# Attention masks of the first of 16 graphs: written by the scalar engine, or added by TensorE

## The chip, the core and the metric

The kernel runs on one NeuronCore of a Trainium2 chip. The metric is the device time of one execution in microseconds (us). A profile is one such execution, recorded instruction by instruction.

TensorE (PE) multiplies a stationary operand with a moving one and writes to the accumulation memory, PSUM. ScalarE (ACT), VectorE (DVE) and GpSimd (POOL) do elementwise work, and SP issues most transfers.

## What is computed

There are 16 graphs (`B`) of 1024 nodes with 128 features. Four residual layers follow each other, each of the form x = x + layer(relu(layernorm(x))): a dilated GraphSAGE layer, softmax attention with a mask, graph attention (GAT), and a graph convolution (GCN). The change concerns the second layer, with four heads of 32 features:

```python
scores = jnp.einsum('chqd,chkd->chqk', q, k) * SCALE
scores = scores + jnp.log(jnp.maximum(edge_weight, EPS))[:, None, :, :]
attn = jax.nn.softmax(scores, axis=-1)
out = jnp.einsum('chqk,chkd->chqd', attn, v)
```

`edge_weight` is the adjacency matrix of zeros and ones, and EPS is 1e-8. A pair without an edge thus gets log(1e-8) = -18.42 more than one with an edge. The kernel adds 16 times the adjacency to the scores and multiplies by SIGMA = 18.42/16 inside the exponential; a constant common to all pairs cancels in the softmax.

## The kernel before, in words

The first part of the kernel (dilation and the three GraphSAGE convolutions) runs up to about 1560 us of the profile. The rest is `attentions_plain`, which takes all 16 graphs through the other three layers. It is written as seven Python generators, one for each kind of work:

- `matrices` (line 1308) loads a graph's adjacency row block by row block, turns it into fp8 (line 1318), and checks its symmetry with small matmuls (lines 1329 and 1331) and an activation (line 1335).
- `before` (line 1343) finishes the first layer (matmuls at line 1365, whose inputs `hT_a` and `h_a` come from HBM by SP's queue), normalises, transposes (line 1291), and makes the queries and keys (line 1383 on PE, 1385 on ACT) and the values (line 1303 on PE, 1387 on ACT).
- `attend` (line 1397) makes the masked scores and their exponentials.
- `values` (line 1434) multiplies the exponentials with the values and with ones (line 1452), takes the reciprocal of the sums (line 1458) and projects.
- `positive` and `gat` (lines 1470 and 1507) are the graph attention: it starts with a normalisation (line 1282) once the graph's softmax attention is done, builds 32 masks on DVE (line 1503) and sums on PE (lines 1563 and 1578).
- `gcn` (line 1602) is the last layer.

For each graph `attend` runs 16 iterations: two halves of the queries (512 columns each) times eight blocks of 128 keys. One iteration fills the tile `s` ("t" in the profile), which is 128 x 4 heads x 512 in fp32. It takes four of PSUM's banks, one for each head, and there is only one such tile. The steps of an iteration are: ACT writes 16 times the adjacency block into all four heads (line 1416); PE adds the scores of the four heads on top (line 1421, four matmuls of 32 rows which lie in different row groups of the array); ACT takes two exponentials of two heads each into `es` ("e" in the profile, two buffers; line 1429). The next iteration's mask can only be written when both exponentials have read `s`. Before the first iteration 16 small identity matmuls (line 1405) write all of `s` once, so that the accumulating matmuls of line 1421 add to what ACT wrote.

`values` (line 1452) issues eight matmuls for each iteration, four with the values and four with ones, in column groups of the array. All other matmul outputs go through two banks named "sum".

The order of the instructions on each engine is made when the program is built. `in_order` (line 1658) steps through the generators. Each yields the engine of its next step, the planned time of the step, and the time at which its inputs are there; the planner always takes the step that can start first, and on a tie prefers the other engines to PE and then the generator with the least PE time done for its weight. The planned time of a mask is 1.9 us on ACT, of a group of scores 1.1 us on PE, of an exponential 1.07 us on ACT, of one iteration's value matmuls 1.95 us on PE. Each engine then works its list strictly in that order and waits wherever an input is late. `matrices` and `before` run ahead of `attend` by up to one graph; so while the first graph is in its attention, the second is being prepared and no GAT or GCN work exists yet.

Of the kernel before, what the change touches and what calls it, by code (L numbers as in the profile page):

```python
# [8 lines left out]
BF16 = mybir.dt.bfloat16  # L9
F8 = mybir.dt.float8e4  # L10
I32 = mybir.dt.int32
AF = mybir.ActivationFunctionType
ALU = mybir.AluOpType
# [5 lines left out]
P = 128  # L19
NB = N // P  # L20
H, HD = 4, 32
HN = N // 2
# [1191 lines left out]
def attentions_plain(tc, x, spill, final, ready_weights, adj, deg, trouble, eye, out, scores, bound, reach):  # L1214
    nc = tc.nc
    with ExitStack() as ctx:
        cp = ctx.enter_context(tc.tile_pool(name="f_const", bufs=1))
# [12 lines left out]
        ident = cp.tile([P, P], F32, name="ident")  # L1230
        nc.sync.dma_start(ident, eye)
        ident16 = cp.tile([P, P], BF16, name="ident16")
# [2 lines left out]
        nc.vector.tensor_scalar(minus16, ident, -1.0, None, op0=ALU.mult)  # L1235
        ones16 = cp.tile([3, P], BF16, name="ones16")
        nc.vector.memset(ones16, 1.0)
        minus_half = cp.tile([P, NB], F32, name="minus_half")
        nc.vector.memset(minus_half, -0.5)
        ones = cp.tile([P, HD], F32, name="ones_hd")  # L1240
# [17 lines left out]
        A, ready, done = {}, {}, {"before": 0, "attend": 0, "gat": 0, "gcn": 0}  # L1258
# [138 lines left out]
        def attend():  # L1397

            last = 0.0


            s = pss.tile([P, H, HN], F32, name="t")
            for hd in range(H):
                for c in range(4):
                    nc.tensor.matmul(s[:, hd, c * P:(c + 1) * P], ident16, ident16, start=c == 0, stop=c == 3)
            n = 0
            for b in range(B):
                while b not in ready or b not in A:
                    yield
                t, xt, qT, kT, va = ready[b]  # L1410
                for hf in range(2):
                    cols = slice(hf * HN, (hf + 1) * HN)
                    for k in range(NB):
                        e = yield "ACT", 1.9, last, 0

                        nc.scalar.activation(s, A[b][:, k, None, cols].to_broadcast([P, H, HN]), AF.Copy, scale=16.0)  # L1416
                        e = yield "PE", 1.1, max(e, t), 0

                        for hd in range(H):
                            r = slice(hd * HD, (hd + 1) * HD)  # L1420
                            nc.tensor.matmul(s[:, hd], kT[r, k * P:(k + 1) * P], qT[r, cols], start=False, stop=True,  # L1421
                                             skip_group_check=True)
                        while n > 1 and n - 2 not in taken:
                            yield
                        es = ep.tile([P, H, HN], F32, name="e")
                        e = max(e, taken.get(n - 2, 0.0))
                        for hd in range(0, H, 2):
                            e = yield "ACT", 1.07, e, 0
                            nc.scalar.activation(es[:, hd:hd + 2], s[:, hd:hd + 2], AF.Exp, scale=SIGMA)  # L1429
                        exps[n] = es, e  # L1430
                        last = e
                        n += 1
# [215 lines left out]
        with tc.manual_schedule(engines=set(ENGINES.values())):  # L1648
            in_order([(0, 4.0, matrices()), (3, 18.0, before()), (0.5, 17.6, attend()), (3, 34.0, values()), (1, 2.0, positive()),
                      (1, 54.0, gat()), (2.5, 17.0, gcn())], {"sum": 2})  # L1650
# [97 lines left out]
def whole(tc, x, adj, nodemask, chunk_mats, chunk_mask, eye, sel, p, out):  # L1748
    nc = tc.nc
    with tc.tile_pool(name="dram", bufs=1, space=DRAM) as dp, tc.tile_pool(name="keep", bufs=1) as kp:  # L1750
# [19 lines left out]
        with tc.tile_pool(name="final", bufs=1) as fp:  # L1770
            final = [fp.tile([P, D], F32, name=f"final{i}") for i in range(3)] + [fp.tile([3, D], BF16, name="final_row")]
            with tc.tile_pool(name="early", bufs=1) as yp, tc.tile_pool(name="c_adj", bufs=2) as ap, \
                    tc.tile_pool(name="c_x", bufs=2) as xp:
                ident = yp.tile([P, P], F32, name="ident")
                nc.sync.dma_start(ident, eye)
                minus_half = yp.tile([P, NB], F32, name="minus_half")
                nc.vector.memset(minus_half, -0.5)
                h0 = xp.tile([P, NB, D], F32, name="xt")
                attention_weights(tc, ap, ident, ready_weights, *weights)
                dilate_plain(tc, adj, eye, kept, rdeg, unsettled, norm_first(tc, x, yp, h0, minus_half))  # L1780
                convolutions_plain(tc, x, ident, ap, xp, h0, minus_half, kept, rdeg, spill, final, *layer0)
            attentions_plain(tc, x, spill, final, ready_weights, adj, deg, trouble, eye, out, scores, bound, reach)
# [45 lines left out]
```

## Time and profile before

| | |
|---|---|
| Median of three runs | 3990.11 us (3984.71 to 3998.74) |
| Profiled execution | 3983.57 us |
| Its span | 3981.8 us |
| Mean granted TensorE clock | 0.932 of full |
| PE, ACT, DVE busy | 86%, 60%, 63% of the span |
| Mask activations (line 1416) | 256, 1883 ns each, first at 1609.6, last at 3825.5 |
| Score matmuls (line 1421) | 1024, recorded as 2048, 663 ns each |
| Exponentials (line 1429) | 512, 1022 ns each |
| Value matmuls (line 1452) | two kinds of 1024 each, recorded as 2048, 620 and 599 ns each |

A row of the profile names line, engine and operation, the tiles (output, arrow, inputs), the shape, and how many there were. Behind the bar stand the busy time in all, the mean of one in ns, and the idle time of the engine just before such instructions with what ended it. An fp32 matmul is recorded as two instructions. The four matmuls of a row or column group run at the same time, so their mean durations can't be multiplied by their number. A line of the timeline gives start, duration, engine, line, operation, tiles, shape and count; a bracket tells how long the engine had been idle and what it waited for.

The second part of the kernel has three stretches: a start (about 1555 to 1725 us) with only the preparation and attention of graph 0, the preparation of graph 1 and its first iterations; a middle, up to about 3830, in which the attention of one graph runs beside the GAT and GCN of earlier ones; and an end, in which GAT and GCN of the last graph remain.

### The profile page before, as it was taken

What the parts mean: (1) busy time and instruction counts of PE and PEld (TensorE: products, weight loads), DVE (VectorE), ACT (ScalarE), POOL (GpSimd) and SP (SyncE); (2) the same over time, 40 slices, a digit from 0 to 9 for tenths busy, and PEclk for the clock granted to TensorE, in tenths of its full rate; (3) what the DMA queues carried; (4) which work ended last, traced back from release to release, by engine and by line L of the source; (5) the groups of instructions that cost most, each with busy time, mean ns of one, the idle gap of its engine ahead of it and who ended that gap; (6) DMA issues with size and microseconds to landing.
All of it is one profiled execution on the core that took longest, in us unless ns stands there. A gap on an engine that the chain in (4) does not pass through costs nothing.

```text
span 3981.8 us, 65726 instructions
## 1 busy us (share of the span) xinstructions
PE 3429.2 (86%) x26692; PEld 1966.6 (49%) x26692; DVE 2528.4 (63%) x4782; ACT 2398.6 (60%) x3961; POOL 790.9 (20%) x680
## 2 busy tenths in 40 slices
PE   4888887899999986789899898998989899889775
PEld 2556565445555565335554544544444454454333
DVE  4988784553344444247775777677687686777656
ACT  3778764453333345776677676767757767776540
POOL 6545421210010011102121111111111101210110
PEclk9989986999999997999999998998999989999887
DMA  9632223443333314211221122122122112111000
GB/s 107 41 21 16 12 79 122 160 170 122 127 128 129 129 61 141 79 59 49 65 86 59 49 75 76 37 75 79 41 67 81 48 50 85 56 58 49 27 17 17
DMA packets 182499, 293.20 MB, mean 74 GB/s; under 512 B 77468, under 2 KB 124456, under 8 KB 173992
## 3 DMA queue, kind: packets, MB, share of 16 engines
q1 hardware_dynamic: 91944, 221.69, 17.1%
q0 software_dynamic: 79728, 24.66, 7.6%
q10 hardware_dynamic: 10512, 42.54, 2.7%
q8 instruction: 211, 3.46, 0.4%
q14 instruction: 104, 0.85, 0.1%
HBM read 287.98 MB, written 51.19 MB: 85 GB/s over the span
## 4 chain that ended last, share of the span: by engine, by line
PE 60%; DVE 20%; ACT 8%; DMA 5%; issue 3%; POOL 3%; ACTq 0%; SPq 0%; POOLq 0%; DVEq 0%
PE g L1040 12%; PE acc L1452 10%; PE sum L1578 9%; PE t L1421 5%; PE sum L1632 4%; PE sum L1563 4%; DVE pm L1503 3%; DMA rows<-in_adj_dram 2%; DVE rows L882 2%; PE sum L1365 2%; PE o L1089 2%; DVE r L835 2%; PE o L1090 2%; ACT e L1429 1%; PE sum L1383 1%
## 5 line engine op out<-in xcount | busy, mean ns | idle before, releaser
L1429 ACT ACTIVATE e<-t 128x1024 f32<-128x1024 f32 x512 | 507.9, 1022 | 485.8 <-PE t L1421 467.9
L1503 DVE SCALAR_TENSOR_TENSOR pm<-dst,minus,A 128x1024 fp8e4<-128x1024 f32 x512 | 675.5, 1348 | 8.4 <-DMA dst<-scores 8.3
L1040 PE MATMUL g<-C,parts 128*128 128x512 fp8e4 x2304 | 523.9, 382 | 15.9 <-DVE aggT L1042 10.0
L1416 ACT ACTIVATE t<-A 128x2048 f32<-128x2048 fp8e4 x256 | 482.0, 1883 | 3.9 <-ACT dst L1483 0.3
L1578 PEld LDWEIGHTS <-pm 128*128 128x128 fp8e4 x4096 | 346.6, 98 | 187.0 <-issue 165.0
L1578 PE MATMUL sum<-parts,pm 128*128 128x198 bf16 x4096 | 399.7, 251 | 26.1 <-DVE pm L1503 16.4
L1452 PE MATMUL acc<-e,va 128*32 128x512 f32 x2048 | 331.6, 620 | 41.1 <-ACT e L1429 38.2
L1040 PEld LDWEIGHTS <-parts 128*128 128x128 bf16 x2304 | 224.0, 99 | 264.1 <-issue 9.6
L1421 PE MATMUL t<-qT,kT 32*128 32x512 f32 x2048 | 303.5, 663 | 30.6 <-ACT t L1416 30.3
L1452 PE MATMUL acc<-e,ones_hd 128*32 128x512 f32 x2048 | 318.4, 599 | 0.0
L1581 DVE TENSOR_REDUCE pos<-sum 128x132 f32<-128x396 f32 x256 | 144.8, 566 | 201.1 <-PE sum L1578 200.5
L1563 PE MATMUL sum<-parts,A 128*128 128x396 bf16 x1024 | 212.1, 352 | 44.9 <-DVE parts L1555 24.0
L1042 DVE TENSOR_TENSOR aggT<-g,rdb 128x512 f32<-128x512 f32 x96 | 66.1, 690 | 270.6 <-PE g L1040 270.5
L1632 PE MATMUL sum<-A,gparts 128*128 128x512 fp8e4 x768 | 176.3, 382 | 24.9 <-ACT gparts L1615 17.6
L1045 POOL TENSOR_TENSOR nrm<-nrm,minus_half 128x8 f32<-128x8 f32 x48 | 78.6, 1638 | 594.3 <-DVE nrm L1103 585.9
L835 DVE TENSOR_TENSOR r<-ya,both 128x512 bf16<-128x512 f16 x184 | 140.4, 777 | 87.9 <-ACT ya L832 87.0
L1275 POOL TENSOR_TENSOR ln_st<-ln_st,minus_half 128x8 f32<-128x8 f32 x48 | 86.1, 1794 | 510.5 <-DVE ln_st L1273 348.4
L1563 PEld LDWEIGHTS <-A 128*128 128x128 fp8e4 x1024 | 94.7, 99 | 183.7 <-issue 106.6
L882 DVE SCALAR_TENSOR_TENSOR rows<-y,thirty,rows 128x1024 fp8e4<-128x1024 f16 x128 | 168.5, 1324 | 24.0 <-ACT y L874 23.5
L1100 ACT ACTIVATE sq<-o 128x512 f32<-128x512 f32 x96 | 55.2, 596 | 204.7 <-PE o L1093 125.1
L872 PE MATMUL big<-tri,rows 128*128 128x256 fp8e4 (+3 forms) x896 | 175.6, 318 | 0.6 <-ACT y L874 0.4
L885 POOL TENSOR_TENSOR own<-rows,lower 128x256 bf16<-128x256 fp8e4 x128 | 109.1, 862 | 334.2 <-DVE rows L882 201.2
(291 smaller groups left out, 6779.7 us busy)
## 6 DMA issues: line engine op xcount, KB each, us to landing
a<-in_adj_dram SPq DMA_DIRECT2D x128, 512.0 KB
C<-kept SPq DMA_DIRECT2D x48, 1024.0 KB
dst<-scores SPq DMA_DIRECT2D x64, 512.0 KB
rdb<-rdeg SPq DMA_DIRECT2D x48, 512.0 KB
spill<-hT ACTq DMA_DIRECT2D x48, 512.0 KB
kept<-rows ACTq DMA_DIRECT2D x16, 1024.0 KB
h_a<-spill SPq DMA_DIRECT2D x64, 256.0 KB
hT_a<-spill SPq DMA_DIRECT2D x16, 512.0 KB
```

The costliest lines, as they stand in the source:

```text
L835: nc.vector.tensor_tensor(r, ya, both[:, 1, :, None].to_broadcast([P, G, P]), op=ALU.is_equal)
L872: nc.tensor.matmul(ps[:, k * P:], lhs, triF[:, :HN - k * P], start=k == 0, stop=k == 3)
L882: nc.vector.scalar_tensor_tensor(row, y16, hh[:, g:g + 1], row, op0=ALU.not_equal, op1=ALU.mult, saturate=False)
L1040: nc.tensor.matmul(ps, parts[:, k, j, :], C[:, j, cols], start=j == 0 and k == 0, stop=j == NB - 1 and k == 2)
L1416: nc.scalar.activation(s, A[b][:, k, None, cols].to_broadcast([P, H, HN]), AF.Copy, scale=16.0)
L1421: nc.tensor.matmul(s[:, hd], kT[r, k * P:(k + 1) * P], qT[r, cols], start=False, stop=True, skip_group_check=True)
L1429: nc.scalar.activation(es[:, hd:hd + 2], s[:, hd:hd + 2], AF.Exp, scale=SIGMA)
L1452: nc.tensor.matmul(ps[r], ones if one else va[:, k, r], es[:, hd], start=k == 0, stop=k == NB - 1)
L1503: nc.vector.scalar_tensor_tensor(pm[:, i, :], dst[hd], minus[:, i, hd:hd + 1], A[b][:, i, :], op0=ALU.is_ge, op1=ALU.mult, saturate=False)
L1563: nc.tensor.matmul(ps[:, :3 * H * W], A[b][:, i, j * P:(j + 1) * P], parts4[:, i, :, :, W:], start=i == 0, stop=i == NB - 1)
L1578: nc.tensor.matmul(ps[:, jj * 6 * W:(jj + 1) * 6 * W], pm[:, i, (j + jj) * P:(j + jj + 1) * P], flat(parts4[:, i, hd]), start=i == 0, stop ...
L1632: nc.tensor.matmul(ps, parts[:, k, m, :], A[b][:, m, cols], start=m == 0 and k == 0, stop=False)
```

## The change

For the first graph (b = 0) the mask is no longer written by ACT. The score matmuls open their banks with start=True, and then four matmuls, one for each head, add the adjacency block (fp8, 128 x 512, as moving operand) times a stationary matrix `ident_log`, which is 16 times the identity in bf16. For all other graphs the mask stays with ACT as before. The planner is told of one PE step of 2.0 us in place of 1.9 us on ACT and 1.1 us on PE. The 16 opening identity matmuls are dropped. One DVE instruction makes `ident_log`.

```diff
+        ident_log = cp.tile([P, P], BF16, name="ident_log")
+        nc.vector.tensor_scalar(ident_log, ident, 16.0, None, op0=ALU.mult)
...
             s = pss.tile([P, H, HN], F32, name="t")
-            for hd in range(H):
-                for c in range(4):
-                    nc.tensor.matmul(s[:, hd, c * P:(c + 1) * P], ident16, ident16, start=c == 0, stop=c == 3)
...
-                        e = yield "ACT", 1.9, last, 0
-
-                        nc.scalar.activation(s, A[b][:, k, None, cols].to_broadcast([P, H, HN]), AF.Copy, scale=16.0)
-                        e = yield "PE", 1.1, max(e, t), 0
+                        if b:
+                            e = yield "ACT", 1.9, last, 0
+                            nc.scalar.activation(s, A[b][:, k, None, cols].to_broadcast([P, H, HN]), AF.Copy, scale=16.0)
+                            e = yield "PE", 1.1, max(e, t), 0
+                        else:
+                            e = yield "PE", 2.0, max(last, t), 0
 
                         for hd in range(H):
                             r = slice(hd * HD, (hd + 1) * HD)
-                            nc.tensor.matmul(s[:, hd], kT[r, k * P:(k + 1) * P], qT[r, cols], start=False, stop=True,
-                                             skip_group_check=True)
+                            nc.tensor.matmul(s[:, hd], kT[r, k * P:(k + 1) * P], qT[r, cols], start=not b, stop=b > 0,
+                                             skip_group_check=b > 0)
+                        if b == 0:
+                            for hd in range(H):
+                                nc.tensor.matmul(s[:, hd], ident_log, A[b][:, k, cols], start=False, stop=True)
```

## The prediction, made before the changed kernel ran

> **What bounds the kernel now.** I read the page's span and busy shares first, then the scalar engine's timeline where the first graph's attention begins, then PE's timeline there, then the windows, then the later graphs.
>
> ```profile
> span 3981.8 us, 65726 instructions
> PE 3429.2 (86%) x26692; PEld 1966.6 (49%) x26692; DVE 2528.4 (63%) x4782; ACT 2398.6 (60%) x3961; POOL 790.9 (20%) x680
> ...
> L1416 ACT ACTIVATE t<-A 128x2048 f32<-128x2048 fp8e4 x256 | 482.0, 1883 | 3.9 <-ACT dst L1483 0.3
> ```
>
> PE is the engine closest to full over the whole span, so taking scalar work away and adding PE work looks like the wrong trade. The share is an average, however. This is the scalar engine in the middle of the first graph's attention (start, duration, engine, line, tiles, then idle time and who ended it):
>
> ```profile
> 1665.66 1.88 ACT L1416 ACTIVATE t<-A 128x2048 f32<-128x2048 fp8e4 x1
> 1668.86 1.94 ACT L1429 ACTIVATE e<-t 128x1024 f32<-128x1024 f32 x2 [1.32 <-PE t L1421]
> 1670.83 1.88 ACT L1416 ACTIVATE t<-A 128x2048 f32<-128x2048 fp8e4 x1
> ```
>
> One iteration is 5.17 us (1670.83 - 1665.66): mask 1.88, a wait of 1.32 for the scores, exponentials 1.94. PE in the same place:
>
> ```profile
> 1664.76 1.54 PE L1452 MATMUL acc<-e,va 128*32 128x512 f32 x6 [1.20 <-ACT e L1429]
> ...
> 1667.59 1.14 PE L1421 MATMUL t<-qT,kT 32*128 32x512 f32 x8
> ...
> 1669.93 1.54 PE L1452 MATMUL acc<-e,va 128*32 128x512 f32 x6 [1.20 <-ACT e L1429]
> ```
>
> Two loops close together here. The scalar one: mask, scores, exponentials. The PE one: scores, 1.20 of idling until the first exponential has landed, then the value matmuls of the same iteration, stretched to 2.83 us (1664.76 to 1667.59) because half of them wait for the second exponential. The mask ends at 1667.54, the value matmuls let go at about the same time, and the next scores start at 1667.59. Removing the mask alone would therefore leave the PE loop; the order on PE must change too.
>
> ```profile
> 1610.00:1655.00 45.00, 35.77 (x214) 16.20 (x218) 11.17 (x30) 33.53 (x54) 5.64 (x3) 0.92 0.29 93
> 1655.00:1712.00 57.00, 42.53 (x271) 9.95 (x264) 5.12 (x4) 42.27 (x35) 0.00 (x0) 1.00 0.03 10
> ...
> 2050.00:2350.00 300.00, 273.73 (x2093) 144.95 (x2096) 217.72 (x313) 216.20 (x288) 49.38 (x25) 0.98 0.21 67
> ```
>
> The columns are the stretch, its length, then PE, weight loads, vector, scalar, POOL, the granted clock, DMA share and GB/s. From 1655 to 1712 nothing but this loop runs: PE 75% busy, scalar 74%, vector nearly idle, hardly any DMA. Later stretches are another regime: PE is 91% busy (273.73 of 300), since the graph attention of one graph fills PE's gaps beside the softmax attention of the next. So the change touches the one stage in which PE has room.
>
> **What the skill says.** "TensorE: Matmul & The Clock Gate", section "Back-to-back issue gap": N/2.4 + 2.5 ns, thus 216 ns for 512 columns on a warm array. The trace agrees: the identity times fp8 mask matmul of line 1329 starts at 1619.08 and its successor at 1619.30, 0.22 us. "ScalarE: Activation LUTs", section "What ACT_TABLE_LOAD costs": 186 ns plus 0.833 ns an element, 1892 ns for 2048; the row shows 1883. "PSUM — Partial Sum Buffer", section "The four PSUM rules": only TensorE sets the written bits. So the first graph's own start matmuls can replace the 16 opening identity matmuls; the bits they leave serve the later graphs. No run here shows the bits themselves.
>
> **The change, part by part.** *Opening.* The 16 identity matmuls (line 1405, 1560.4 to 1562.3) go and one vector scaling of the identity is added; the like one at line 1235 took 0.21 us. Both lie where the engines await the first adjacency row, which the scalar engine gets at 1568.29 after 13.62 us of idling. Nothing, and 0.2 us if that cover were gone.
>
> *Pure iteration.* Away: 1.88 us of mask. New: four matmuls of 0.22 us. The listed order of PE's instructions also changes: before, scores(n), values(n), scores(n+1); after, scores(n+1), masks(n+1), values(n), so that values run under the next exponentials. The scalar loop: scores 1.07 (from 1618.00 to the next instruction at 1619.08); the first exponential needs two heads, so one mask start 0.22 and one mask's length 0.39; hop 0.13 (1657.25 + 1.14 to 1658.52); exponentials 1.94; 0.05 to the next scores. Sum 3.80. The PE loop: 1.07 + 4 x 0.22 + values unstretched 1.86 (1625.97 to 1627.83) + 0.1 for changing array shape = 3.91. So PE becomes the limit, at about 3.9: 1.27 saved per iteration. PE has then no gap.
>
> *First iterations.* In the trace PE waits for two loads of graph 1:
>
> ```profile
> 1613.56 0.49 PE L1365 MATMUL sum<-final,hT_a 128*128 128x128 f32 x2 [3.74 <-DMA hT_a<-spill]
> ...
> 1618.00 1.14 PE L1421 MATMUL t<-qT,kT 32*128 32x512 f32 x8
> ...
> 1622.17 0.49 PE L1365 MATMUL sum<-final,h_a 128*128 128x128 f32 x2 [2.17 <-DMA h_a<-spill]
> ...
> 1627.83 1.14 PE L1421 MATMUL t<-qT,kT 32*128 32x512 f32 x8
> ```
>
> In the new order only one group of six line-1365 matmuls stands ahead of the first scores, so they start at 1614.9, not 1618.0. But before the second scores stand the six of graph 1's second half, and these need `h_a`, whose transfer starts when the first half's matmuls end, and takes some 4.2 us (1618.0 to 1622.17). Those end near 1619.5 now, the data lands near 1623.8, and the second scores start near 1625.3 instead of 1627.83. Behind this wait PE's whole loop is queued, and the scalar engine's exponentials with it. Gain 2.5.
>
> *Iterations 1 to 15.* Before, graph 1's preparation lay partly in the loop's gaps. With no gap on PE all of it counts; after the second scores, from the rows of 1618 to 1657: the symmetry matmuls (lines 1329, 1331) 3.0 in all (seven groups, 0.53 for the largest, 1625.44 to 1625.97), one 1365 group 1.34, eight transposes 1.0, four line-1383 matmuls 3.9, eight of line 1303 2.3 (twice 1.16); 11.5, taken as 12. I add 2 where an eight-fold normalisation of 3.18 and two row activations stand between two exponentials (scalar limits there), and 1.6 where the values of the second half wait for the 3.36 us reciprocal, which exceeds the 1.95 until PE comes to them. Then the last exponential ends at 1625.3 + 14 x 3.9 + 3.75 + 12 + 2 + 1.6 = 1699.3. It was 1712.4. So the stage gives 13.1 us. Bounds: 8 if PE pays for array-shape changes and half-clock windows (0.3 an iteration); 20 if the preparation hides as before (16 x 1.27).
>
> *What is late next.* The end of attention 0 lets the reciprocal, projection, and normalisation of line 1282 follow (1726.9). In both listed orders 18 iterations stand ahead of that, and as many preparation steps, so it moves by the whole 13.1. From there PE is the limit, its work is unaltered, and a shift stays. What comes in addition is the new order itself: the planner re-times everything, and the listed orders differ in detail through all 16 graphs. Trace of before: line 1282's normalisations of successive graphs lie 141.8 apart on average, between 133.8 and 151.3. Per-graph spread of some 5 us, largely repaid by the neighbour; I take 0 with an allowance of 8 either way. The tail (1282 of the last graph at 3854.1 to the end, PE 58% busy) has the same instructions.
>
> *Sum.* The profiled execution took 3983.57, span 3981.8. 3983.6 - 13.1 = 3970.5. The median of the three runs, 3990.11, lies 6.5 above; so the median comes to 3977.
>
> **Rivals.** *Swallowed*: the shift is taken back by waits downstream, on `h_a` transfers or on PE's queue order. For: 23 us of PE waits on `h_a` after 1760. Against: these loads are triggered by PE's own progress and so move along. Gains 3: 3987. *More than I count*: preparation hides and the new order is luckier: 22: 3968. *Slower*: the new order for the 15 other graphs is worse. One mechanism: the mask of a later graph is put where PE waits for it. In the PE waits from 1760 to 3830 that is the largest item:
>
> ```profile
> PE t L1421 <- ACT t L1416: 30.3, 20, 4.0
> PE sum L1303 <- DVE oT L1460: 29.5, 7, 9.1
> ```
>
> If the mean period goes from 141.8 to over 142.7 (13.1 / 15 = 0.87), the gain is gone; at +1.75, 3990 - 13 + 26 = 4003. Against it: nothing makes the new order worse in kind. *The change doing nothing*: excluded, since the listed order shows 240 mask activations and 64 mask matmuls.
>
> **How the numbers follow.** What a measurement can tell from no change is 0.3%, 12 us. Likeliest (0.50): the stage's gain arrives, 3966 to 3988 with the re-ordering; 0.36 of it beyond 12 us, 0.14 within. More: 0.24, all faster. Swallowed: 0.16, same. Slower: 0.10. Faster 0.60, same 0.30, slower 0.10. The range 3956 to 3994 leaves out the slower case and the far edge of the larger one.
>
> **What would show it right or wrong.** The first graph's pure iterations at 3.9 us with PE gapless; scores 0 near 1615, scores 1 near 1625; the last exponential of graph 0 at about 1699; line 1282 at about 1714; period still 141.8. Wrong if iterations stay above 4.6 (the array's change of shape costs), or if the normalisation is early by 13 and the end isn't.

## The result, and the profile after

| | Before | Changed |
|---|---|---|
| Median of seven runs | 3987.81 us | 3974.86 us |
| Lowest to highest | 3982.88 to 3998.74 | 3969.86 to 3982.53 |
| Ratio, with its 95% interval | 1 | 0.9971 (0.9957 to 0.9985) |
| Profiled execution, span | 3983.57, 3981.8 | 3979.43, 3977.7 |

The changed kernel is 13 us faster, as forecast: 3977 was predicted, from 3956 to 3994. In ratio that is 0.29%, at the very edge of the 0.3% that the prediction called faster.

The page of the changed kernel, its span, busy times, and the mask activation (now line 1417; line numbers move by 1 to 6, so 1282 is 1284, 1365 is 1367, 1421 is 1424, 1429 is 1435, 1452 is 1458, and the new mask matmuls are line 1428):

```profile
span 3977.7 us, 65816 instructions
...
PE 3432.1 (86%) x26740; PEld 1968.0 (49%) x26740; DVE 2524.4 (63%) x4783; ACT 2367.1 (60%) x3945; POOL 796.4 (20%) x680
...
L1417 ACT ACTIVATE t<-A 128x2048 f32<-128x2048 fp8e4 x240 | 452.0, 1883 | 3.6 <-ACT dst L1489 0.3
```

Sixteen mask activations are gone. ACT is 31 us less busy and PE 3 us more. The page alone doesn't show where time was won. This is ACT's timeline in the middle of graph 0's attention (start, duration, what; in brackets the idle time and who ended it):

```profile
1687.98 1.94 ACT L1435 ACTIVATE e<-t 128x1024 f32<-128x1024 f32 x2 [2.26 <-PE t L1428]
1692.18 1.94 ACT L1435 ACTIVATE e<-t 128x1024 f32<-128x1024 f32 x2 [2.26 <-PE t L1428]
```

An iteration takes 4.20 us (1692.18 - 1687.98) where it took 5.17. PE's timeline in the same place:

```profile
1689.97 1.14 PE L1424 MATMUL t<-qT,kT 32*128 32x512 f32 x8 [0.23 <-ACT e L1435]
1691.05 1.04 PE L1428 MATMUL t<-A,ident_log 128*128 128x512 fp8e4 x4
1692.01 1.06 PE L1458 MATMUL acc<-e,va 128*32 128x512 f32 x8
1692.89 1.04 PE L1458 MATMUL acc<-e,ones_hd 128*32 128x512 f32 x8
1694.17 1.14 PE L1424 MATMUL t<-qT,kT 32*128 32x512 f32 x8 [0.23 <-ACT e L1435]
```

Scores, masks, and values follow each other, and one gap of 0.23 us is left ahead of the scores. The values run under the exponentials and are no longer stretched. The window over the middle of the stage (length, PE, weight loads, DVE, ACT, POOL, clock, DMA) has PE almost full:

```profile
1655.00:1699.00 44.00, 43.06 (x297) 13.74 (x295) 6.46 (x5) 22.80 (x29) 0.00 (x0) 1.00 0.08 26
```

The traces can be cut at marks that every kernel has: the last store of the convolutions ("spill"), the first line-1365 matmul of graph 1 that waits for `hT_a`, the end of graph 0's last exponential, the normalisation of line 1282 for graph 0 and for graph 15, and the end. All in us, computed from the starts of these instructions:

| Kernel | start to spill | hT_a to last exp. | hT_a to norm. 0 (the stage) | norm. 0 to 15 | norm. 15 to end | norm. 0 to end |
|---|---|---|---|---|---|---|
| before | 1554.7 | 98.9 | 113.3 | 2127.2 | 127.7 | 2254.9 |
| changed | 1560.8 | 86.9 | 101.4 | 2112.9 | 143.5 | 2256.4 |
| changed_again | 1547.4 | 86.2 | 102.4 | 2112.0 | 143.2 | 2255.2 |
| old_order | 1552.9 | 110.0 | 125.3 | 2128.7 | 127.4 | 2256.1 |
| order_alone | 1552.2 | 96.3 | 112.1 | 2126.5 | 128.1 | 2254.6 |
| later_order_kept | 1553.6 | 86.4 | 101.8 | 2121.4 | 127.5 | 2249.0 |
| kept_again | 1550.2 | 86.2 | 101.3 | 2129.1 | 127.5 | 2256.6 |
| two_score_tiles | 1552.7 | 82.8 | 99.0 | 2110.1 | 143.3 | 2253.4 |
| tiles_without_change | 1553.2 | 101.3 | 115.8 | 2120.4 | 127.6 | 2248.0 |
| both_refinements | 1550.5 | 84.4 | 99.0 | 2114.2 | 127.6 | 2241.7 |
| told_2_3 | 1549.1 | 86.6 | 101.2 | 2091.8 | 140.3 | 2232.1 |
| told_1_8 | 1549.1 | 84.8 | 99.4 | 2141.5 | 128.3 | 2269.8 |
| told_2_3_two_tiles | 1548.3 | 84.5 | 99.0 | 2085.5 | 139.2 | 2224.6 |
| all_graphs | 1547.8 | 85.8 | 105.8 | 2268.1 | 135.4 | 2403.4 |

The first two rows tell the story. The stage is 11.9 us shorter; the stretch after it is the same (+1.5). The part ahead of the change, which both kernels share, happened to be 6.1 us longer in the changed kernel's profiled execution, so that its span shows only 4 of the 12 us.

### The profile page after: what moved, and what is told of

It reads as the page before. It is cut to its first block, busy times and chain, and to the rows that moved or that the text cites. A ratio compares the mean times of both kernels' runs of the same rounds, so it can differ in the third digit from the quotient of the medians.

```text
span 3977.7 us, 65816 instructions
## 1 busy us (share of the span) xinstructions
PE 3432.1 (86%) x26740; PEld 1968.0 (49%) x26740; DVE 2524.4 (63%) x4783; ACT 2367.1 (60%) x3945; POOL 796.4 (20%) x680
## 4 chain that ended last, share of the span: by engine, by line
PE 60%; DVE 20%; ACT 8%; DMA 5%; POOL 3%; issue 3%; ACTq 0%; SPq 0%; POOLq 0%; DVEq 0%
PE g L1040 12%; PE acc L1458 9%; PE sum L1584 9%; PE t L1424 5%; PE sum L1638 4%; PE sum L1569 4%; DVE pm L1509 3%; DMA rows<-in_adj_dram 2%; PE sum L1367 2%; DVE rows L882 2%; DVE r L835 2%; PE o L1089 2%; PE o L1090 2%; ACT e L1435 1%; DVE rden L1464 1%
## 5 line engine op out<-in xcount | busy, mean ns | idle before, releaser
L1417 ACT ACTIVATE t<-A 128x2048 f32<-128x2048 fp8e4 x240 | 452.0, 1883 | 3.6 <-ACT dst L1489 0.3
L1458 PE MATMUL acc<-e,va 128*32 128x512 f32 x2048 | 316.2, 621 | 12.6 <-ACT e L1435 12.1
L1458 PE MATMUL acc<-e,ones_hd 128*32 128x512 f32 x2048 | 302.7, 599 | 0.0
L1593 POOL TENSOR_TENSOR pos<-pos,ex 128x1056 f32<-128x1056 f32 x16 | 43.6, 2724 | 703.5 <-DVE pos L1587 703.5
```

The source lines that it names most:

```text
L1458: nc.tensor.matmul(ps[r], ones if one else va[:, k, r], es[:, hd], start=k == 0, stop=k == NB - 1)
```

## The experiments

Every kernel was timed beside the kernel before on the same chip, and its ratio to that time is given. Kernels that were not timed side by side are compared by these ratios.

### Is it the mask taken from ACT, or the order on PE?

*old_order* has the new matmuls but tells the planner the old steps, so that everything else stands in the old order:

```diff
-                        if b:
-                            e = yield "ACT", 1.9, last, 0
+                        e = yield "ACT", 1.9, last, 0
+                        if b:
                             nc.scalar.activation(s, A[b][:, k, None, cols].to_broadcast([P, H, HN]), AF.Copy, scale=16.0)
-                            e = yield "PE", 1.1, max(e, t), 0
-                        else:
-                            e = yield "PE", 2.0, max(last, t), 0
+                        e = yield "PE", 1.1, max(e, t), 0
```

> The new instructions in the old order: the masks of graph 0 are added by TensorE, but the planner is told the old steps (1.9 us on ACT, then 1.1 us on PE), so every other instruction stands where it stood before, with the value matmuls of an iteration ahead of the next scores. My theory is that the gain needs the changed order on PE. One pure iteration of graph 0 is then scores and masks up to the first exponential 2.21 us, its exponential until the values can begin 1.07, stretched values 2.83: 6.11 us, longer than the 5.17 of before. Stage from the arrival of hT_a to the normalisation of line 1282 about 120 us (before 113.3, changed kernel 101.4); time about 8 us above the kernel before, some 3996 us. The rival, that taking ACT's 1.88 us away is what pays, expects a pure iteration of 4.2 us or at least below 5.17, and a time at the changed kernel's 3975 us.

Measured: 3993.05 us, ratio 1.0020 (1.0012 to 1.0029), slower than before; the stage is 125.3 us, where about 120 was expected. PE's and ACT's timelines of this kernel, in which the two lines of ACT give the iteration:

```profile
1681.46 1.14 PE L1422 MATMUL t<-qT,kT 32*128 32x512 f32 x8
1682.53 1.04 PE L1426 MATMUL t<-A,ident_log 128*128 128x512 fp8e4 x4
1684.74 1.54 PE L1456 MATMUL acc<-e,va 128*32 128x512 f32 x6 [1.17 <-ACT e L1433]
```

```profile
1683.66 1.94 ACT L1433 ACTIVATE e<-t 128x1024 f32<-128x1024 f32 x2 [4.10 <-PE t L1426]
1689.70 1.94 ACT L1433 ACTIVATE e<-t 128x1024 f32<-128x1024 f32 x2 [4.10 <-PE t L1426]
```

An iteration is 6.04 us. ACT idles 4.10 us of it, and PE still idles 1.17 while the values wait for the exponential of their own iteration. With 1.88 us less work on ACT the loop became longer, because in the old order the loop that matters goes through PE, and the four masks lengthen it: 6.04 - 5.17 = 0.87 us, and 4 x 0.22 = 0.88. The rival is out.

*order_alone* is the opposite half: masks on ACT, values of graph 0 behind the next scores.

```diff
-        exps, taken = {}, {}
+        exps, taken, scored = {}, {}, set()
...
                                              skip_group_check=True)
+                        scored.add(n)
...
-                        while n not in exps:
+                        while n not in exps or n < 15 and n + 1 not in scored:
```

> The masks stay on ACT for all graphs, but the value matmuls of graph 0 are put behind the next iteration's scores, as in the changed kernel. My theory: the loop over ACT (mask 1.88, wait 1.32, exponentials 1.94, in all 5.17 us) is then alone the limit, so a pure iteration stays at 5.17 us, the stage at about 113 us and the time at that of the kernel before (3988 us) within the re-ordering's 8 us. The rival, that the order alone pays, expects below 4.5 us an iteration and some 10 us less.

Measured: 3979.27 us, ratio 0.9990 (0.9980 to 0.9999); iterations of 5.17 us, stage 112.1. On ACT:

```profile
1669.27 1.88 ACT L1416 ACTIVATE t<-A 128x2048 f32<-128x2048 fp8e4 x1
1672.47 1.94 ACT L1430 ACTIVATE e<-t 128x1024 f32<-128x1024 f32 x2 [1.32 <-PE t L1421]
1674.44 1.88 ACT L1416 ACTIVATE t<-A 128x2048 f32<-128x2048 fp8e4 x1
```

The same 1.88, 1.32 and 1.94 as before. Neither half shortens the iteration; both together save 0.97 us of it. The 5 us that this kernel does gain lie outside the pure iterations, and what gave them was not traced further.

### The 0.3 us that the iteration is longer than predicted

*two_score_tiles* cuts the tile `s` in two, so that an instruction on heads 0 and 1 no longer shares a tile with one on heads 2 and 3:

```diff
-            s = pss.tile([P, H, HN], F32, name="t")
+            two = [pss.tile([P, 2, HN], F32, name=f"t{i}") for i in range(2)]
...
-                            nc.scalar.activation(s, A[b][:, k, None, cols].to_broadcast([P, H, HN]), AF.Copy, scale=16.0)
+                            for s in two:
+                                nc.scalar.activation(s, A[b][:, k, None, cols].to_broadcast([P, 2, HN]), AF.Copy, scale=16.0)
...
-                            nc.scalar.activation(es[:, hd:hd + 2], s[:, hd:hd + 2], AF.Exp, scale=SIGMA)
+                            nc.scalar.activation(es[:, hd:hd + 2], two[hd // 2], AF.Exp, scale=SIGMA)
```

> The changed kernel with the score tile cut into two tiles of two heads each, in all graphs (the mask activation of later graphs becomes two of half the size); the order is unaltered. In the changed kernel a pure iteration takes 4.20 us, not the 3.9 of my sum, and the first exponential starts after the last of the four masks, where I had let it start after the second. My theory: it waits for the whole tile. With two tiles it starts two masks earlier (0.44 us), PE closes its gap of 0.23 us, and a pure iteration takes 3.97 us; the stage becomes 2 to 4 us shorter than 101.4. In the later graphs ACT pays about 0.1 us more for each of 240 masks, which is hidden; time 3972 us. The rival, that the exponential waits for something else (the array's drain, a hop), expects 4.20 us as before.

Measured: 3962.92 us, ratio 0.9952 (0.9936 to 0.9969). On PE:

```profile
1681.68 1.14 PE L1425 MATMUL t<-qT,kT 32*128 32x512 f32 x8
1682.75 1.04 PE L1429 MATMUL t<-A,ident_log 128*128 128x512 fp8e4 x4
1683.72 1.06 PE L1459 MATMUL acc<-e,va 128*32 128x512 f32 x8
1684.60 1.04 PE L1459 MATMUL acc<-e,ones_hd 128*32 128x512 f32 x8
1685.57 1.14 PE L1425 MATMUL t<-qT,kT 32*128 32x512 f32 x8
```

No gap is left: 3.89 us an iteration (1685.57 - 1681.68; 3.97 was expected), the stage 2.4 us shorter. On ACT:

```profile
1683.45 1.94 ACT L1436 ACTIVATE e<-t 128x1024 f32<-128x1024 f32 x2 [1.96 <-PE t L1429]
```

The exponential starts at 1683.45, 1.77 us after the scores and not 2.21 (1692.18 - 1689.97), while the last of the four masks still runs. So the 0.23 us gap was the first exponential waiting for a whole tile. The cut loosens a second wait too: scores of heads 0 and 1 could now start before the second exponential has read heads 2 and 3. That freedom is not used here, since both exponentials end at 1685.39 (1683.45 + 1.94), ahead of the next scores at 1685.57. The ratio is 0.0019, or 7.6 us, below the changed kernel's 0.9971; the stage explains 2.4 of it, and with overlapping intervals the rest is not shown.

*tiles_without_change* applies the same cut to the kernel before.

> The kernel before with only the score tile cut into two tiles of two heads; masks on ACT, the order as before. My theory: in the old order the loop over PE (scores, one exponential, values stretched to 2.83 us) holds a pure iteration at about 5.1 us whatever the first exponential waits for, so graph 0's stage stays at 113 us and the time within 5 us of the kernel before. The rival, that the wait for the whole tile costs in the old kernel too, expects a pure iteration of 4.7 us or less and a stage at least 5 us shorter.

Measured: 3978.81 us, ratio 0.9986 (0.9978 to 0.9995); iterations of 5.07 us (1671.55 - 1666.48), stage 115.8. On ACT:

```profile
1666.48 1.94 ACT L1430 ACTIVATE e<-t 128x1024 f32<-128x1024 f32 x2 [1.27 <-PE t L1422]
1671.55 1.94 ACT L1430 ACTIVATE e<-t 128x1024 f32<-128x1024 f32 x2 [1.27 <-PE t L1422]
```

In graph 0 the cut takes no more than 0.10 us off an iteration under the old order, as expected, and the stage is not shorter. The few us of the ratio come from elsewhere; in the profile the stretch after the stage is 2248.0 us, 6.9 below before. The finer wait pays in the first graph only after the change has made the first exponential the last thing that PE waits for.

### What the new order does to the other 15 graphs

*later_order_kept* follows the changed order up to the last exponential of graph 0 and then the old one. `ORDER` is the list of 4720 step numbers, one digit for the generator of each:

```diff
+    every = list(jobs)
+    for c in script or ():
+        j = every[int(c)]
+        tries = 0
+        while j["next"] is None:
+            j["next"], tries = next(j["job"]), tries + 1
+            assert tries < 3, c
+        try:
+            j["next"] = j["job"].send(0.0)
+        except StopIteration:
+            jobs.remove(j)
```

> The changed kernel up to the last exponential of graph 0; from there all engines follow the order of the kernel before, written out step by step, so that the planner's new order for the other 15 graphs is gone. My theory: the gain is that of the stage, about 12 us in the profile, and the new order is worth about nothing. Expected: the stretch from the normalisation of line 1282 to the end 2255 us as before (2254.9; changed kernel 2256.4), with its two parts as before: 2127 to the last graph's normalisation and 128 after it (changed kernel 2113 and 143); time 3976 us, within 5 us of the changed kernel. The rival, that the new order gives or takes a good part, expects 6 us or more between the two.

Measured: 3966.68 us, ratio 0.9960 (0.9945 to 0.9975). Its parts after the stage have the proportions of before (127.5 us after the last normalisation), so it is the new order that moved 16 us across that mark. The sum was 2249.0, 6 us below what I expected. To see whether that was real, the changed kernel and this one ran again.

> The changed kernel once more, beside the next kernel and the kernel before on one chip. In its first profile the part ahead of the change, which both kernels have in common, was 6.1 us later than in that of before (last spill at 1560.8, not 1554.7). My theory: that is chance of the run. Expected: the part ahead of the change near 1553, as in the four profiles since, hence a span near 3970; the stage from hT_a to line 1282's normalisation 101 to 102 us again, the rest 2256 us; about 13 us below the kernel before. The rival, that the change itself delays the earlier part, expects 1560 again.

> The kernel that keeps the later order, once more, beside two kernels with other orders. It had a ratio of 0.9960 to the kernel before, the changed kernel 0.9971 and 0.9974, with overlapping intervals; in the profiles the stretch from line 1282's normalisation of graph 0 to the end was 2249.0 against 2256.4 and 2255.2. If the planner's new order costs some 6 us, this comes out at 0.996 again and the stretch near 2249; if the difference was chance (a kernel with the same later order, the old order with the new instructions, had 2256.1), ratio near 0.997 and stretch near 2255.

Measured: changed_again 3972.44 us, ratio 0.9974 (0.9965 to 0.9984), with the part ahead at 1547.4 and the stretch after the stage at 2255.2; kept_again 3967.31 us, ratio 0.9951 (0.9933 to 0.9969), with a stretch of 2256.6. The same program thus shows 2249.0 and 2256.6 in two executions, as large a spread as the difference in question. By the profiles the new order is worth nothing; by the ratios (0.9971 and 0.9974 against 0.9960 and 0.9951) it costs 4 to 9 us, with intervals that overlap. A third pair, both_refinements below against two_score_tiles (0.9932 and 0.9952), points the same way. So a cost of some us is likely, but no single pair is clear of its interval, and its size stays open. And the 1560.8 of the first profile was not the change's doing: the twelve later profiles, all of kernels with the same program up to there, lie between 1547.4 and 1553.6.

*told_2_3* and *told_1_8* leave every instruction of the changed kernel as it is and alter one number in the planner, so that the order alone differs:

```diff
-                            e = yield "PE", 2.0, max(last, t), 0
+                            e = yield "PE", 2.3, max(last, t), 0
```

> The changed kernel, with the planner told 2.3 us instead of 2.0 for the scores and masks of graph 0; no instruction is added or removed, and the order differs through all later graphs. My theory: re-timing is a lottery of some 8 us either way. Expected: stage 100 to 104 us, the stretch after it between 2245 and 2265 us, ratio between 0.995 and 0.999. The rival, that the order of later graphs matters little, expects 2255 us within 2 us, ratio 0.997.

> The same with 1.8 us. My theory: again somewhere between 2245 and 2265 us after the stage, and not the same as with 2.0 or 2.3. The rival: 2255 us within 2 us.

Measured: told_2_3 3948.54 us, ratio 0.9905 (0.9886 to 0.9925); told_1_8 3980.38 us, ratio 0.9988 (0.9975 to 1.0001). The stages are alike (101.2 and 99.4), but the stretch after it is 2232.1 and 2269.8, both outside what I had given. The sums over the windows from 1760 to 3830 us show the same thing on PE. In this order, before, changed kernel, told 2.3, told 1.8:

```profile
sum 2070.00, PE 1841.56 PEld 974.67 DVE 1493.36 ACT 1403.68 POOL 327.05; mean PE 263.08 PEld 139.24 DVE 213.34 ACT 200.53 POOL 46.72
```

```profile
sum 2070.00, PE 1844.62 PEld 972.28 DVE 1492.10 ACT 1399.45 POOL 326.99; mean PE 263.52 PEld 138.90 DVE 213.16 ACT 199.92 POOL 46.71
```

```profile
sum 2070.00, PE 1863.11 PEld 990.61 DVE 1489.28 ACT 1404.09 POOL 333.78; mean PE 266.16 PEld 141.52 DVE 212.75 ACT 200.58 POOL 47.68
```

```profile
sum 2070.00, PE 1834.76 PEld 970.16 DVE 1475.28 ACT 1389.07 POOL 325.29; mean PE 262.11 PEld 138.59 DVE 210.75 ACT 198.44 POOL 46.47
```

The PE work is the same in the last three kernels. The order that packs 1863 us of it into these 2070 is 22.8 us shorter after the stage than before, the one that packs 1835 is 14.9 us longer. The change's own order packs 3 us more than before, and is about neutral. The windows are fixed in time, so this is a rough measure: told_2_3 has its last normalisation at 3801 us, before they end.

The wait that the prediction named, PE waiting for the mask of a later graph, does not tell the better order from the worse. It was 30.3 us before; in the changed kernel, told 2.3 and told 1.8 it is (total in us, times, longest, from 1760 to 3800 us):

```profile
PE t L1424 <- ACT t L1417: 43.4, 18, 7.0
PE t L1424 <- ACT t L1417: 48.1, 20, 4.0
PE t L1424 <- ACT t L1417: 43.0, 20, 4.3
```

The fastest order has the most of it. Which waits decide stays open.

### The limits of the trade, and the refinements together

*all_graphs* lets TensorE add the masks of all 16 graphs, and ACT writes none.

> The masks of all 16 graphs by TensorE; ACT writes none. My theory: in the later graphs PE is the limit (91% busy), so most of the added 240 x 4 x 0.22 = 211 us of PE comes on top, less some 30 us in which PE had waited for ACT's masks and some idle gaps: 150 to 210 us longer, near 4160 us, while ACT becomes 450 us less busy. The rival, that PE's idle 9% takes the masks in, expects less than 60 us more.

Measured: 4122.12 us, ratio 1.0347 (1.0332 to 1.0362), 138 us slower. Lines of its page:

```profile
span 4114.6 us, 67437 instructions
...
PE 3624.4 (88%) x27700; PEld 2036.8 (50%) x27700; DVE 2521.8 (61%) x4783; ACT 1942.9 (47%) x3705; POOL 796.3 (19%) x680
```

PE became 192 us busier than in the changed kernel (3624.4 - 3432.1), ACT 424 us less busy, and about three quarters of PE's addition (some 150 of 192, by the ratios 1.0347 and 0.9971) came out as time. I had expected 150 to 210 us above before. In the profiles PE's idle time fell by 55 us (span less busy time, 545.6 to 490.2), more than I thought, and the mean granted clock was 0.946 and not 0.933; what each of the two is worth was not separated. The sign of the trade is that of the stage: a gain where PE has room, a loss where it is the limit.

*both_refinements* joins later_order_kept and two_score_tiles, *told_2_3_two_tiles* the better order and the two tiles.

> The changed kernel with the order of the kernel before kept for the other 15 graphs, and with the score tile in two tiles of two heads. If the two act in different places they add: stage 99 us, the rest 2249 us or a little less, so 2 to 4 us below the kernel that keeps the later order alone: ratio to the kernel before near 0.995. If the later order was no gain, the ratio is that of two tiles alone, 0.9952, within its interval. The rival, that two tiles paid by the accident of a new timing, expects no gain over the later order kept alone, 0.996.

> The kernel with the planner told 2.3 us, with the score tile in two tiles of two heads. The two act in different places and should add: a pure iteration of 3.89 instead of 4.20 us, stage near 99 us instead of 101.2, the stretch after it at or a few us below 2232, ratio to the kernel before 0.987 to 0.990, thus below both kernels. The rival, that the good order is upset by any shift of some us, expects the stretch back at 2240 us or more.

Measured: 3955.16 us, ratio 0.9932 (0.9918 to 0.9946), and 3940.07 us, ratio 0.9890 (0.9874 to 0.9907). Both stages are 99.0. both_refinements came out below the 0.995 that was expected, with 2241.7 us after the stage and not 2249; what gave that is not shown. The last one is the fastest kernel of this study, 1.1% below the kernel before: some 14 us from the stage, the rest mostly from an order that was found by altering one number.

## Why the prediction was right, point by point

- **The bound.** Right: two loops of equal length in graph 0's attention, and the order on PE as a condition. old_order (6.04 us; 6.11 was expected from the same terms) and order_alone (5.17) show each half failing by itself.
- **Opening.** Right. From the spill to `hT_a` it took 58.9 us before and 59.0 after.
- **Pure iteration.** The failed term is "the first exponential needs two heads, so one mask start 0.22 and one mask's length 0.39". It needs the whole tile, thus two more mask starts. ACT's loop is 3.80 + 0.44 = 4.24 by that, measured 4.20, and not PE's 3.91 was the limit. With two tiles it is 3.89.
- **First iterations.** Half right. Graph 0's first scores came 1.8 us after `hT_a` (predicted 1.3), the second ones 13.1 after (predicted 11.7; before 14.3). So 1.2 us were gained, not 2.5. The data of `h_a` was in time, 10.0 us after `hT_a` (predicted 10.2). What took longer is PE's work behind the two waits, for which the prediction counted full clock. The granted clock was 0.55 from 1619.8 to 1623.6, and the first scores took 2.01 us and not 1.14; it was 0.57 from 1629.85 to 1632.92, and from `h_a` to the second scores 3.07 us passed and not 1.5. The kernel before has such a stretch too (granted 0.62 from 1613.5 to 1618.0), but its first scores stood behind it. The amount varies: in changed_again the second scores came 11.8 us after `hT_a`, as predicted.

```profile
1619.83 0.62 PE L1367 MATMUL sum<-final,hT_a 128*128 128x128 f32 x2 [3.66 <-DMA hT_a<-spill]
...
1621.66 2.01 PE L1424 MATMUL t<-qT,kT 32*128 32x512 f32 x8
...
1629.85 0.49 PE L1367 MATMUL sum<-final,h_a 128*128 128x128 f32 x2 [3.17 <-DMA h_a<-spill]
...
1632.92 1.50 PE L1424 MATMUL t<-qT,kT 32*128 32x512 f32 x8
```

- **Iterations 1 to 15.** From the second scores to the last exponential's end 73.8 us, predicted 74.0 (1699.3 - 1625.3); but that is luck, since two errors cancel. Fourteen iterations of 4.20 and a last one of 4.15 (scores and masks 2.21, exponentials 1.94) make 63.0, so the preparation cost 10.8 and not 15.6. The 0.23 us gaps leave room for some of it, and no wait for the reciprocal shows, since matmuls of lines 1383 and 1303 stood in its place; how the 4.8 us divide was not measured.
- **The stage.** Predicted 13.1, measured 11.9 and 10.9 in two profiles.
- **What is late next.** The shift arrived. "Has the same instructions" was wrong of the tail: the new order left more of graph 14's last layer for it (143.5 us in place of 127.7), and 14.3 less came ahead. The sum is unaltered.
- **The new order.** Taken as 0, and measured as such in the profiles, within a spread of 8 us between executions of one program; by the ratios it costs some us. But the allowance of "8 either way" was too small: one number in the planner moved that stretch by -22.8 and +14.9. That this change got a nearly neutral order was luck, and could not be read from the profile; a range of the changed kernel's time that takes in orders of this kind would have been some 40 us wide for this term alone.
- **Rivals.** Swallowed: no. More than counted: no, the stage gave 11.9 us and not 22. Slower by the order of later graphs: not in this kernel, but told_1_8, whose ratio of 0.9988 is only 5 us below before though its stage won 14, shows that an order can take back more than half of the gain. The mechanism given for it, later masks for which PE waits, is not borne out (43.0 us there, 43.4 in the changed kernel, 48.1 in the fast told_2_3).

## What to carry to other kernels

Read the bound of the stage that a change touches, not of the kernel: PE was the fullest engine over the span and yet had a quarter of its time free in this stage. When work is moved to another engine, ask which loop closes last and where the next instruction stands in the new engine's queue; here the transfer alone made things worse, and the order alone left the iteration at 5.17 us. And where a planner writes static queues, price its re-ordering as a term of its own: run the same instructions with a few different orders before believing a gain of half a per cent, and take the best one.

## What the runs showed of the hardware

- TensorE added a fp8 mask block to fp32 scores in PSUM at 0.22 us for 128 x 512 (from the first of four masks to the next matmul of the full array 0.88, 1640.22 to 1641.10 in the changed kernel), directly behind four matmuls in row groups of the array. From the scores' start to the masks' start 1.07 us passed, the same as ahead of other matmuls.
- Where the next matmuls lay in another shape of the array, some 0.09 us more passed: from the masks' start to that of the values in column groups 0.97 us and not 0.88, and from the second group of value matmuls to the next scores 0.97 (1684.60 to 1685.57 with two tiles) where one such group follows the other after 0.88 (1683.72 to 1684.60).
- PE was 98% busy at full granted clock (43.06 of 44 us, clock 1.00) in the changed stage, while after a wait of 3.66 us for a transfer the granted clock was 0.55, and the same matmuls took 2.01 us instead of 1.14.
